# Second phase of a transformer kernel: the 64-row block of the MLP moved behind the scores, residual additions moved with it, one attention output a step later, one small exponential earlier

## The chip, the cores and the metric

The kernel runs on one core of one Trainium2 chip, as one launch. The metric is the device time in microseconds (us) of that core, the median of several runs. The core's engines are TensorE (PE in the profile, its weight loads PEld), VectorE (DVE), ScalarE (ACT), GpSimd (POOL) and SyncE (SP), which issues the DMAs.

## What is computed

The reference takes `x` of 8 x 1024 x 256 in float32 and adds two blocks to it, each on a layer norm of its input:

```python
x = x + attn(layernorm(x))          # latent attention, 16 heads, causal: first phase
x = x + ffn(layernorm(x))           # two layers of the following: second phase

def layer(x):
    q, k, v = split(shift_token(x) @ wqkv)            # 8 heads of 64
    q, k = rotary_xpos(l2norm(q) * qs, l2norm(k) * ks)
    x = x + local_attention(q, k, v) @ wo             # windows of 128, each sees itself and the one before
    h = layernorm(shift_token(x)) * lg + lb
    a, g = split(h @ w1 + b1)                         # 682 columns each
    return x + (a * gelu(g)) @ w2 + b2
```

The change touches the second phase alone, and there the order of work, not what is computed.

## The kernel before

The first phase (function `mla`) ends a little after 950 us of the span; the second (`local`) takes the rest.

**Passes, windows, chunks.** `local` goes through 16 passes (`passes`, L1049): two layers of eight batches. A pass has 8 windows of 128 tokens (attention works on these) and two chunks of 512 tokens (the MLP works on these), so there are 128 windows and 32 chunks.

**One loop of steps.** The order of PE, DVE, ACT and POOL is written out by hand: inside `tc.manual_schedule` (L1209) each of these engines does its instructions in the order of the program text. SP isn't in that list; its order is chosen when the program is built. The loop of L1210 makes one step per window, and in each step works on several windows at different stages (`each(step, name, back)` calls a method of the pass for the window `back` steps ago):

- `both` (L981, 4 back): on DVE, sums of the exponentials of a window and its predecessor, later added up over keys by PE;
- `qk` (L886, this window): PE multiplies into one of two double banks of PSUM, `pair`, that are taken in turn (`turns`, L869) by `qk` and by each of the two halves of `scores`; ACT squares (L897), DVE multiplies by tables (L899, L902), reduces (L908, L909), POOL adds and scales (L906, L911, L912);
- `transposes` (L923, 1 back): DVE turns 32x32 blocks (L930), and SP writes them to DRAM and reads them back as `qkT` (L933, L937);
- `v` (L915): PE, then a copy by ACT;
- a unit of the MLP, `next(units)` (L1227);
- `values` (L990, 4 back): PE forms `o` (L1003) and the sums `s` (L1011); DVE takes the reciprocal of `s` (L1015), a sum for a later test (L1019), the product `oT` (L1020) and another sum (L1024);
- `scores` (L945, 3 back): PE, with 64 rows of contraction and 32 columns per matmul (L962), in two halves; ACT takes the exponential of each half (L968); POOL masks (L970, L975). The last window of a pass has half as many columns;
- in every second step `output` (L1028, two windows, 6 and 5 back): PE multiplies by `wo` into `psw`, DVE adds to the residual `x_` (L1037), SP writes `y` (L1040, L1042) and after a whole chunk reads `h` back (L1047);
- another unit of the MLP (L1238).

**The MLP as a generator.** `mlp` (L1097) yields eight units a chunk, two of them per step, so a chunk takes four steps. Units 1 to 5 are `up` for a gate and a value (tile `ag`, PE, 64 matmul instructions), then the gelu by ACT (L1127) and the product `hid` by DVE (L1128). Unit 6 is `up` for the last 42 columns of both, with its gelu (L1137) and `rest_hid` (L1142), and the norm of the next chunk. Unit 7 (L1149 to L1173) multiplies by `w2` into two banks, `psy`: first 128-row matmuls from `hid` (160 instructions), then those of the 64-row block from `rest_hid` (32 instructions), whose two row halves serve the two banks; then DVE adds each bank to the residual `x_` (L1165), and SP writes it to `xs` (first layer), or DVE adds `x2` as well (L1171) and SP writes `out` (second layer). Unit 8 scales the next chunk's `d` by ACT (L1091). Unit 7 is always the first unit of its step. It stands ahead of `values`, and `output` stands behind `scores` in that same step, because both come every fourth and every second step.

**Buffers.** The pool of PSUM banks tagged `mm` has three (`psum3`, L673): `pv`, `ag`, `psy`, `psw` and `s` share them. `pair` has two, `acc` (for `o`) one. The bank of a tile is handed on once its readers are done.

**Streams.** In steps 3 to 7 of a pass, `ahead` (L1186) loads and turns the input of the next pass (`turneds`, L804, on DVE; eight `xT` DMAs on SP). In the first layer it also norms it.

Of the kernel before, what the change touches and what calls it, by code (L numbers as in the profile page):

```python
# [82 lines left out]
def preln_mla_local_kernel(  # L83
# [574 lines left out]
    def local(ctx: ExitStack, verdict):  # L658
# [212 lines left out]
        class Pass:  # L871
# [3 lines left out]
            def __init__(self, n, l, b, w, x_, xT):  # L875
                self.n, self.l, self.b, self.w, self.x_, self.xT = n, l, b, w, x_, xT
                self.y = ys[n % 3]
                self.hs, self.rot, self.vs, self.pts, self.oTs = {}, {}, {}, {}, {}

            def key(self, i):  # L880
                return f"{self.b}_{self.l}_{i}"
# [107 lines left out]

            def values(self, i):  # L990

                key, vs, pts, oTs = self.key(i), self.vs, self.pts, self.oTs
                blocks = [(i - 1, P)] if i else []
                blocks.append((i, 0))
                o = pacc.tile([P, 2, 2, P], F32, tag="acc", name=f"o{key}")
                s = psum.tile([P, 2, P], F32, tag="mm", name=f"s{key}")
                place = lambda j: 2 * (j % 2) + j // 2
                for g in range(2):
                    for a in range(2):
                        for m, off in blocks:  # L1000
                            for j in range(4):
                                h = 4 * g + j
                                nc.tensor.matmul(  # L1003
                                    o[32 * j : 32 * j + 32, g, a, :],
                                    vs[m][:, h * DH + a * 32 : h * DH + a * 32 + 32],
                                    pts[m][g][:, place(j), off : off + P],
                                    start=(m == blocks[0][0]), stop=(m == i),
                                )
                for g in range(2):
                    for j in range(4):  # L1010
                        nc.tensor.matmul(  # L1011
                            s[32 * j : 32 * j + 32, g, :], ones, self.sums[g][:, place(j), :], start=True, stop=True
                        )
                rs = p1.tile([P, 2, P], F32, tag="lrs", name=f"rs{key}")
                nc.vector.reciprocal(rs, s)  # L1015
                if i % 2 == 0:
                    oTs[i // 2] = p2.tile([P, 4, 2 * P], F32, tag="oT", name=f"oT{key}")
                at = self.n * NT + i
                nc.vector.tensor_reduce(stats[:, 1, at : at + 1], s, AX.XY, ALU.add)  # L1019
                nc.vector.tensor_tensor(  # L1020
                    oTs[i // 2][:, :, (i % 2) * P : (i % 2 + 1) * P].rearrange("p (g a) q -> p g a q", g=2),
                    o, rs.unsqueeze(2).to_broadcast([P, 2, 2, P]), ALU.mult,
                )
                nc.vector.tensor_reduce(stats[:, 0, at : at + 1], rs, AX.XY, ALU.add)  # L1024
                if i:
                    del vs[i - 1], pts[i - 1]
# [23 lines left out]
        made = {}  # L1050
        chunks = [(n, m) for n in range(len(passes)) for m in range(NCH)]
        ds, found = {}, {}

        def look_at_chunk(k):
            if k < len(chunks):
# [41 lines left out]
        def mlp():  # L1097


            w = load_mlp(0)  # L1100
            yield
            look_at_chunk(0)
            yield
            norm_chunk(0)
            turn_chunk(0)
            yield
            scale_chunk(0, w)
            for k, (q, n) in enumerate(chunks):
                l, b, x_ = made[q].l, made[q].b, made[q].x_
                key = made[q].key(n)  # L1110
                d = ds.pop(k)

                def up(i):
                    ps = psum.tile([P, CH], F32, tag="mm", name=f"ag{key}_{i}")
                    for c in range(2):
                        times(
                            ps.rearrange("p (s a t) -> p s a t", a=4, t=32), w["1"][:, c, i, :], d[:, c],
                            c == 0, c == 1,
                        )
                    return ps  # L1120

                hid = p1.tile([P, NF, CH], F32, tag="hid", name=f"hid{key}")
                for i in range(NF):
                    gate = up(2 * i + 1)
                    a = up(2 * i)
                    ge = p2.tile([P, CH], F32, tag="ge", name=f"ge{key}_{i}")
                    nc.scalar.activation(ge, gate, AF.Gelu, bias=w["b1"][:, 2 * i + 1 : 2 * i + 2])  # L1127
                    nc.vector.scalar_tensor_tensor(  # L1128
                        hid[:, i, :], a, w["b1"][:, 2 * i : 2 * i + 1], ge, ALU.add, ALU.mult
                    )  # L1130
                    if i + 1 == NF:
                        look_at_chunk(k + 1)
                    yield
                both = up(2 * NF)
                ge = p2.tile([P, CH], F32, tag="ge", name=f"ge{key}_{NF}")
                last = slice(2 * NF, 2 * NF + 1)
                nc.scalar.activation(  # L1137
                    ge[:REST], both[64 : 64 + REST], AF.Gelu, bias=w["b1"][64 : 64 + REST, last]
                )
                for g in range(2):  # L1140
                    cols = slice(CH // 2 * g, CH // 2 * (g + 1))
                    nc.vector.scalar_tensor_tensor(  # L1142
                        rest_hid[64 * g : 64 * g + REST], both[:REST, cols], w["b1"][:REST, last],
                        ge[:REST, cols], ALU.add, ALU.mult,
                    )
                norm_chunk(k + 1)
                turn_chunk(k + 1)
                yield
                if l + 1 == DEPTH:  # L1149
                    xt = load_x2(b, n)  # L1150
                sums = [psum.tile([P, 2, D], F32, tag="mm", name=f"psy{key}_{g}") for g in range(2)]
                for g, ps in enumerate(sums):
                    for t in range(2):
                        cols = slice((2 * g + t) * P, (2 * g + t + 1) * P)
                        for i in range(NF):
                            times(ps[:, t, :], hid[:, i, cols], w["2"][:, i, :], t == i == 0, False)
                for t in range(2):
                    for g, ps in enumerate(sums):
                        rows = slice(64 * g, 64 * g + 64)
                        times(  # L1160
                            ps[:, t, :], rest_hid[rows, t * P : (t + 1) * P], w["2"][rows, NF, :], False, t == 1
                        )
                for g, ps in enumerate(sums):
                    part = slice(ST * n + 2 * g, ST * n + 2 * g + 2)
                    nc.vector.tensor_tensor(x_[:, part], ps, x_[:, part], ALU.add)  # L1165
                    if l + 1 < DEPTH:
                        nc.sync.dma_start(xs[b][:, part], x_[:, part])
                    else:
                        rows = slice(n * CH + 2 * g * P, n * CH + (2 * g + 2) * P)
                        both = xt[:, 2 * g : 2 * g + 2]  # L1170
                        nc.vector.tensor_tensor(both, x_[:, part], both, ALU.add)  # L1171
                        nc.sync.dma_start(out[b, rows].rearrange("(t p) d -> p t d", p=P), both)
                yield  # L1173
                if k + 1 < len(chunks) and made[chunks[k + 1][0]].l > l:
                    w = load_mlp(l + 1)
                scale_chunk(k + 1, w)
                yield
# [24 lines left out]
        def each(step, name, back):  # L1202
            j = step - back
            if 0 <= j < windows:
                n, i = divmod(j, NT)
                getattr(made[n], name)(i)

        E = mybir.EngineType
        with tc.manual_schedule(engines={E.PE, E.DVE, E.Activation, E.Pool}):  # L1209
            for step in range(windows + LAG):  # L1210
# [12 lines left out]
                each(step, "transposes", 1)  # L1223
                if not late:
                    each(step, "v", 0)
                if step >= LAG:
                    next(units, None)  # L1227
                if NT - 2 <= i and step < windows:
                    ahead(n + 1)
                each(step, "values", 4)  # L1230
                each(step, "scores", 3)
                j = step - 6
                if 0 <= j < windows and j % 2 == 0:
                    made[j // NT].output(j % NT // 2)
                elif 0 <= j < windows - 1 and (j + 1) % (B * NT) == 0:
                    w["o"] = load_o(passes[(j + 1) // NT][0])
                if step >= LAG - 2:
# [5 lines left out]
                if i >= NT - 5 and step < windows:  # L1243
                    got = ahead(n + 1)
                    if got:
                        ready[n + 1] = got
            for _ in units:
                pass

        ok = p1.tile([P, 2, B * DEPTH * NT], F32, name="okl")  # L1250
        for m, top in enumerate((HIGH, 1 / LOW)):
# [612 lines left out]
```

## Time and profile before

| | us |
|---|---|
| median of 3 runs | 3276.89 |
| lowest, highest | 3273.80, 3278.76 |
| the profiled execution | 3275.27 |
| its span, first to last instruction | 3273.5 |

The mean TensorE clock granted was 0.993 of full speed. In the profile, PE's matmuls are pipelined and overlap, so that a block's own cost is read from its start to the start of the next block, not from its length. In the groups by line, the columns are: line, engine, operation, tiles written and read, shapes, count, then busy us and mean ns of one, then idle time of the engine just before such instructions and what ended it. In the waits, they are: who waited, for whom, us in total, times, longest. L670 is the helper `times`, which issues four matmuls of 32 columns each; its blocks are told apart by their tiles.

### The profile page before, as it was taken

To read this page: it belongs to the slowest core of one execution; us is meant where nothing else is said; L and a number is where in the kernel's file an instruction comes from. 1 tells how busy PE (TensorE), PEld (TensorE's weight loads), DVE (VectorE), ACT (ScalarE), POOL (GpSimd) and SP (SyncE) were. 2 spreads that over 40 slices of the span, in tenths; PEclk is the share of its full clock that TensorE was granted. 3 is DMA by queue.
4 is the path that set the end of the run, shared out by engine and by line. 5 is a ranking of instruction groups with operands and counts; after the bars stand their busy time and mean duration, and the time that the engine had idled before them with its cause. 6 is when DMAs were issued, how large, how long until landed. Compare 5 with 4: busy or idle time off the path is not lost.

```text
span 3273.5 us, 112729 instructions
## 1 busy us (share of the span) xinstructions
PE 3177.2 (97%) x50274; PEld 1456.0 (44%) x50274; DVE 2671.1 (82%) x3934; ACT 1712.5 (52%) x2055; POOL 1341.6 (41%) x1064
## 2 busy tenths in 40 slices
PE   7999999999987999999999999999999999999998
PEld 2434343443333445444445444444554444544454
DVE  4999989998987888887888877777877878787773
ACT  6888888888852343444443444444444444444441
POOL 1001000000018655565555555555555555555540
PEclk9999999999998999999999999999999999999999
DMA  4133223323333444544445445444544545454431
GB/s 128 43 95 85 56 75 78 85 53 81 98 98 104 108 129 118 142 111 122 131 115 135 120 131 144 120 130 142 144 131 130 133 122 134 134 140 126 114 106 59
DMA packets 389900, 364.21 MB, mean 111 GB/s; under 512 B 158703, under 2 KB 337310, under 8 KB 389278
## 3 DMA queue, kind: packets, MB, share of 16 engines
q1 hardware_dynamic: 387422, 354.51, 40.1%
q8 instruction: 397, 6.50, 0.8%
q10 hardware_dynamic: 1984, 2.41, 0.2%
q14 instruction: 97, 0.79, 0.1%
HBM read 165.96 MB, written 140.51 MB: 94 GB/s over the span
## 4 chain that ended last, share of the span: by engine, by line
PE 84%; DVE 6%; ACT 4%; DMA 3%; issue 2%; SPq 1%; POOL 0%; ACTq 0%; DVEq 0%; POOLq 0%
PE ag L670 17%; PE pair L670 13%; PE psy L670 9%; PE psw L670 7%; PE acc L488 7%; PE pv L670 6%; PE o L1003 6%; PE sc L455 5%; PE pair L962 4%; DVE pt L477 3%; PE s L1011 2%; PE psx L201 2%; PE psq L201 1%; PE psR L201 1%; ACT pt L463 1%
## 5 line engine op out<-in xcount | busy, mean ns | idle before, releaser
L477 DVE TENSOR_TENSOR pt<-pt,er 128x1024 f32<-128x1024 f32 x576 | 671.9, 1222 | 35.5 <-ACT pt L463 35.5
L670 PE MATMUL ag<-d,l 128*32 128x512 f32 x5632 | 639.8, 593 | 0.7 <-ACT d L1085 0.4
L906 POOL TENSOR_TENSOR t<-t,t 128x1024 f32<-128x1024 f32 x128 | 304.2, 2377 | 780.2 <-DVE t L902 780.2
L463 ACT ACTIVATE pt<-sc 128x1024 f32<-128x1024 f32 x576 | 561.0, 1032 | 115.4 <-PE sc L455 105.6
L968 ACT ACT_TABLE_LOAD x120 | 154.0, 1283 | 686.9 <-PE pair L962 686.8
L670 PE MATMUL pair<-l_qkv,xT 128*32 128x512 f32 x4096 | 468.3, 597 | 6.6 <-ACT pt L968 3.2
L126 POOL TENSOR_TENSOR rn<-ss,half 128x16 f32<-128x16 f32 x128 | 373.4, 2917 | 13.9
L488 PE MATMUL acc<-pt,v 128*32 128x512 f32 (+3 forms) x3072 | 345.6, 497 | 11.1 <-DVE pt L477 10.0
L670 PEld LDWEIGHTS ag<-d,l 128*32 128x32 f32 x5632 | 179.0, 110 | 384.0 <-issue 362.0
L897 ACT ACTIVATE sq<-pair 128x1024 f32<-128x1024 f32 x128 | 131.2, 1025 | 331.0 <-issue 256.0
L899 DVE TENSOR_TENSOR t<-pair,l_cos 128x1024 f32<-128x1024 f32 x128 | 156.3, 1221 | 155.1 <-ACT sq L897 154.8
L670 PE MATMUL psy<-l,hid 128*32 128x256 f32 x5120 | 282.1, 379 | 0.0
L670 PEld LDWEIGHTS pair<-l_qkv,xT 128*32 128x32 f32 x4096 | 132.6, 111 | 307.8 <-issue 252.5
L1128 DVE SCALAR_TENSOR_TENSOR hid<-ag,l_b,ge 128x512 f32<-128x512 f32 x160 | 115.9, 724 | 188.2 <-ACT ge L1127 164.5
L968 ACT ACTIVATE pt<-pair 128x1024 f32<-128x1024 f32 (+1 forms) x256 | 235.1, 969 | 56.4 <-PE pair L962 55.1
L912 POOL TENSOR_TENSOR t<-t,rn 128x1024 f32<-128x1024 f32 x128 | 245.4, 1918 | 10.0
L455 PE MATMUL sc<-q,k 32*128 32x512 f32 (+3 forms) x3072 | 245.2, 380 | 4.0 <-ACT pt L463 3.0
L1003 PEld LDWEIGHTS o<-pt,v 128*32 128x32 f32 x7680 | 212.8, 110 | 72.7 <-issue 68.9
L670 PE MATMUL pv<-l_qkv,xT 128*32 128x512 f32 x2048 | 244.1, 592 | 0.0
L670 PE MATMUL psw<-l_o,oT 128*32 128x256 f32 x4096 | 240.2, 386 | 0.1
L1003 PE MATMUL o<-pt,v 128*32 128x128 f32 x7680 | 235.6, 273 | 1.7 <-POOL pt L970 1.6
L420 POOL TENSOR_SCALAR_AFFINE_SELECT er<-er 128x128 f32<-128x128 f32 x64 | 39.1, 610 | 480.7 <-ACT er L418 480.7
(324 smaller groups left out, 4639.5 us busy)
## 6 DMA issues: line engine op xcount, KB each, us to landing
z<-turned SPq DMA_DIRECT2D x512, 128.0 KB, 2.8
qkT<-z SPq DMA_DIRECT2D x128, 512.0 KB, 3.9
y<-xs SPq DMA_DIRECT2D x128, 128.0 KB, 3.8
h<-y SPq DMA_DIRECT2D x32, 512.0 KB, 4.4
zx<-turneds SPq DMA_DIRECT2D x120, 128.0 KB, 2.8
xT<-zx SPq DMA_DIRECT2D x240, 64.0 KB, 2.9
zh<-turnedh SPq DMA_DIRECT2D x120, 128.0 KB, 2.3
d<-zh SPq DMA_DIRECT2D x30, 512.0 KB, 3.3
```

What stands on the lines that cost most here:

```text
L126: nc.gpsimd.tensor_tensor(out_, in_, half[:, :n], ALU.pow)
L455: nc.tensor.matmul(two[n // 2][:, n % 2, lo : lo + w], k[rows], q[rows, h], start=(h == 1), stop=(h == 0),)
L463: nc.scalar.activation(pt, sc, AF.Exp, scale=SCALE)
L477: nc.vector.tensor_tensor(t, t, er.to_broadcast([P, 1024 // w, w]), ALU.mult)
L488: nc.tensor.matmul(self.acc[g][32 * n : 32 * n + 32, q0 - c * 512 :], self.v[:, kb, h * VW : h * VW + 32], pts[n // 2][:, n % 2, lo : lo + w],
L670: nc.tensor.matmul(out[four], w[:, four], rhs, start=start, stop=stop)
L897: nc.scalar.activation(sq, qk, AF.Square)
L899: nc.vector.tensor_tensor(t1, qk, A[:, i].unsqueeze(2).to_broadcast([P, 2, HEADS, DH]), ALU.mult)
L906: nc.gpsimd.tensor_tensor(t1, t1, t2, ALU.add)
L912: nc.gpsimd.tensor_tensor(t1, t1, rn.unsqueeze(3).to_broadcast([P, 2, HEADS, DH]), ALU.mult)
L968: nc.scalar.activation(pt[:, :, : n * P], flat[:, :, : n * P], AF.Exp, scale=-1.0)
L1003: nc.tensor.matmul(o[32 * j : 32 * j + 32, g, a, :], vs[m][:, h * DH + a * 32 : h * DH + a * 32 + 32], pts[m][g][:, place(j), off : off + ...
```

## The change

Four edits, all in `local`:

1. Unit 7 issues only the 128-row matmuls of `psy`. The 64-row block, the residual additions and their DMAs go into a closure, `rest`, that the step calls behind `scores`.
2. `values` keeps its matmuls; its four DVE instructions become a method `divide`, called behind `rest`. So on DVE the residual additions still stand ahead of the reciprocal, but both now stand behind the scores' place.
3. In a step with a `rest`, `output` is held and called in the next step, behind `v` and ahead of the first unit.
4. Ahead of `scores`, ACT takes the exponential of one zeroed column, `spark`, that nothing reads.

```diff
+                self.done[i] = o, s
+
+            def divide(self, i):
+                key, vs, pts, oTs = self.key(i), self.vs, self.pts, self.oTs
+                o, s = self.done.pop(i)
                 rs = p1.tile([P, 2, P], F32, tag="lrs", name=f"rs{key}")
                 nc.vector.reciprocal(rs, s)
...
-                for t in range(2):
+                def rest(w=w, sums=sums, l=l, b=b, n=n, x_=x_, xt=xt):
+                    for t in range(2):
+                        for g, ps in enumerate(sums):
+                            rows = slice(64 * g, 64 * g + 64)
+                            times(
+                                ps[:, t, :], rest_hid[rows, t * P : (t + 1) * P], w["2"][rows, NF, :], False, t == 1
+                            )
                     for g, ps in enumerate(sums):
-                        rows = slice(64 * g, 64 * g + 64)
-                        times(
-                            ps[:, t, :], rest_hid[rows, t * P : (t + 1) * P], w["2"][rows, NF, :], False, t == 1
-                        )
-                for g, ps in enumerate(sums):
-                    part = slice(ST * n + 2 * g, ST * n + 2 * g + 2)
-                    nc.vector.tensor_tensor(x_[:, part], ps, x_[:, part], ALU.add)
-                    if l + 1 < DEPTH:
-                        nc.sync.dma_start(xs[b][:, part], x_[:, part])
-                    else:
...
+                        part = slice(ST * n + 2 * g, ST * n + 2 * g + 2)
+                        nc.vector.tensor_tensor(x_[:, part], ps, x_[:, part], ALU.add)
+                        if l + 1 < DEPTH:
+                            nc.sync.dma_start(xs[b][:, part], x_[:, part])
+                        else:
+                            rows = slice(n * CH + 2 * g * P, n * CH + (2 * g + 2) * P)
+                            both = xt[:, 2 * g : 2 * g + 2]
+                            nc.vector.tensor_tensor(both, x_[:, part], both, ALU.add)
+                            nc.sync.dma_start(out[b, rows].rearrange("(t p) d -> p t d", p=P), both)
+
+                rests.append(rest)
                 yield
...
+        column = p1.tile([P, 1], F32, name="column_l")
+        nc.gpsimd.memset(column, 0.0)
+        spark = p1.tile([P, 1], F32, name="spark")
...
                 if not late:
                     each(step, "v", 0)
+                while held:
+                    j = held.pop()
+                    made[j // NT].output(j % NT // 2)
                 if step >= LAG:
                     next(units, None)
                 if NT - 2 <= i and step < windows:
                     ahead(n + 1)
                 each(step, "values", 4)
+                if 0 <= step - 3 < windows:
+                    nc.scalar.activation(spark, column, AF.Exp)
                 each(step, "scores", 3)
+                full = bool(rests)
+                while rests:
+                    rests.pop()()
+                each(step, "divide", 4)
                 j = step - 6
                 if 0 <= j < windows and j % 2 == 0:
-                    made[j // NT].output(j % NT // 2)
+                    if full and step + 1 < windows:
+                        held.append(j)
+                    else:
+                        made[j // NT].output(j % NT // 2)
```

More of the change, by code (lines that the diff above doesn't have):

```diff
@@ L877, in __init__ @@
                 self.y = ys[n % 3]
-                self.hs, self.rot, self.vs, self.pts, self.oTs = {}, {}, {}, {}, {}
+                self.hs, self.rot, self.vs, self.pts, self.oTs, self.done = {}, {}, {}, {}, {}, {}
             def key(self, i):
@@ L990, in values @@
             def values(self, i):
-                key, vs, pts, oTs = self.key(i), self.vs, self.pts, self.oTs
+                key, vs, pts = self.key(i), self.vs, self.pts
                 blocks = [(i - 1, P)] if i else []
@@ L1052, in local @@
         ds, found = {}, {}
+        rests, held = [], []
         def look_at_chunk(k):
@@ L1148, in mlp @@
                 yield
-                if l + 1 == DEPTH:
-                    xt = load_x2(b, n)
+                xt = load_x2(b, n) if l + 1 == DEPTH else None
                 sums = [psum.tile([P, 2, D], F32, tag="mm", name=f"psy{key}_{g}") for g in range(2)]
@@ L1156, in mlp @@
                             times(ps[:, t, :], hid[:, i, cols], w["2"][:, i, :], t == i == 0, False)
-                for t in range(2):
-                    for g, ps in enumerate(sums):
-                        rows = slice(64 * g, 64 * g + 64)
-                        times(
-                            ps[:, t, :], rest_hid[rows, t * P : (t + 1) * P], w["2"][rows, NF, :], False, t == 1
-                        )
-                for g, ps in enumerate(sums):
-                    part = slice(ST * n + 2 * g, ST * n + 2 * g + 2)
-                    nc.vector.tensor_tensor(x_[:, part], ps, x_[:, part], ALU.add)
-                    if l + 1 < DEPTH:
-                        nc.sync.dma_start(xs[b][:, part], x_[:, part])
-                    else:
[L1169 to L1172, printed above, removed]
+                def rest(w=w, sums=sums, l=l, b=b, n=n, x_=x_, xt=xt):
[5 more added lines that the diff above has]
+                            )
+                    for g, ps in enumerate(sums):
+                        part = slice(ST * n + 2 * g, ST * n + 2 * g + 2)
[8 more added lines that the diff above has]
+                rests.append(rest)
                 yield
@@ L1246, in local @@
                         ready[n + 1] = got
+                while rests:
+                    rests.pop()()
             for _ in units:
-                pass
+                while rests:
+                    rests.pop()()
         ok = p1.tile([P, 2, B * DEPTH * NT], F32, name="okl")
```

## The prediction

> **What bounds the kernel now.** I read the page first (busy times, then the chain that ended last), then the groups of the second phase by shape, then the timeline of each engine around one step in which the down projection `psy` runs, then the waits.
>
> The page: TensorE (PE) is busy 97% of the span and makes 84% of the chain; VectorE (DVE) is next.
>
> ```profile
> PE 3177.2 (97%) x50274; PEld 1456.0 (44%) x50274; DVE 2671.1 (82%) x3934; ACT 1712.5 (52%) x2055; POOL 1341.6 (41%) x1064
> PE 84%; DVE 6%; ACT 4%; DMA 3%; issue 2%; SPq 1%; POOL 0%; ACTq 0%; DVEq 0%; POOLq 0%
> ```
>
> In the second phase PE issues almost without a hole, so only what makes its blocks start later than their own work demands can be won. The timeline of PE around the nineteenth `psy` (columns: start, length, engine, line, tile, count) shows two such places:
>
> ```profile
> 2417.68 1.92 PE L670 MATMUL ag<-d,l 128*32 128x512 f32 x16
> 2419.73 3.64 PE L670 MATMUL pair<-l_qkv,xT 128*32 128x512 f32 x32
> 2423.19 1.90 PE L670 MATMUL pv<-l_qkv,xT 128*32 128x512 f32 x16
> 2424.91 8.82 PE L670 MATMUL psy<-l,hid 128*32 128x256 f32 x160
> 2433.66 1.09 PE L670 MATMUL psy<-l,rest_hid 64*32 64x256 f32 x32
> 2434.68 1.95 PE L1003 MATMUL o<-pt,v 128*32 128x128 f32 x64
> ...
> 2437.00 1.32 PE L962 MATMUL pair<-qkT 64*32 64x160 f32 x64
> ```
>
> First, 16 matmuls take 1.72 us from start to next start (`pv`, 2423.19 to 2424.91), but the 16 of `ag` at 2417.68 take 2.05 until `pair` starts: 0.33 of waiting. The list of waits names the cause, ScalarE (ACT) reading the pair bank that `qk` will overwrite; the groups show what stands in front of that read:
>
> ```profile
> PEld pair L670 <- ACT pt L968: 37.3, 55, 1.3
> ```
>
> ```profile
> L968 ACT ACT_TABLE_LOAD x120 | 154.0, 1283 | 686.9 <-PE pair L962 686.8
> ```
>
> The table load queues behind the wait for the scores, so each of 120 steps pays 1.28 us between scores and exponential, though ACT was idle before (686.9 us in all).
>
> Second, `psy` runs in 128-row tiles, its rest in 64-row ones. At 53.65 ns a matmul (half of `pv`'s 107.3, for half the columns) 160 take 8.58 us; from `psy` to its rest are 8.75: 0.16 over. The rest's 32 run two row halves at a time, 26.8 ns each, 0.86; up to `o` are 1.02: 0.16 over. A change of tile shape costs about 0.16 each way.
>
> **What the Trainium skill says.** "TensorEngine Tiling (Array Packing)", Key Properties: changing the tiling mode drains TensorE. The trace agrees, with those 0.16 us. "ScalarE: Activation LUTs", What ACT_TABLE_LOAD costs: 1283 ns for the load plus some 1380 for a drain. The 1283 is here; the drain isn't: the load at 2437.93 is followed by the exponential at 2439.22, 1.29 later. "GPSIMD Engine Reference", Specifications: it shares SBUF interfaces with VectorE, and DVE instructions with two SBUF inputs contend. The trace agrees: the residual addition L1171 takes 0.69 us alone and 1.67 beside POOL's L912.
>
> **The change part by part.** There are 32 chunks, so 32 `psy` steps; the last two (of the drain-out) have no scores beside them.
>
> *Early exponential.* It adds one [128,1] exponential per step; the skill's price for an instruction with immediate operands (186 ns, same section; an estimate) makes 0.2 us. It stands after the gelu and ahead of the scores, where ACT idles 4 to 12 us, so it costs nothing; without that cover it would be 128 x 0.2 = 26. The load moves into the idle time and the exponential starts 1.28 earlier. On PE's path this counts only where `qk` waits for it: once per chunk, in the step after which only 16 `ag` matmuls follow the scores. I count 0.31 us (2.05 against 1.74, the shortest case) x 29 (the last such steps have no `qk` after them) = **9.0 us**. Elsewhere 3.4 us of `ag` or 3.5 of `psw` hide it.
>
> *64-row block behind the scores.* Scores are 64-row too, so rest and scores share one change in and one out: 0.16 + 0.16 = 0.33 x 30 = **9.9 us**. Between 0 (if something else makes those 0.16) and 0.35 per chunk; I take 0.33.
>
> *Attention output (`psw`, 64 matmuls) a step later.* The same work; `x_` and `y` get that half chunk 17 us later, and `h`, which reads `y`, waits for the other half, written two steps later. On SP, its two `y` issues move past the next step's four `z` and one `qkT`; the `xs`/`out` issues come with the additions, some 3 us later. The reader of `xs` is chunks away. 0. But `psw` no longer stands between scores and `qk`. Counting from the start of the scores, `qk` now comes at 1.07 + 1.02 = 2.10; the exponential releases the bank at 0.92 + 1.02 = 1.94, which without the early load would be 3.22. Covered, with 0.1 left.
>
> *Additions and reciprocals.* They now wait for the end of the rest. This is where I expect a new stall. DVE in the same step, before:
>
> ```profile
> 2434.79 0.69 DVE L1165 TENSOR_TENSOR xs<-psy,xs 128x512 f32<-128x512 f32 x1 [0.72 <-PE psy L670]
> 2435.51 0.69 DVE L1171 TENSOR_TENSOR x<-xs,x 128x512 f32<-128x512 f32 x1
> 2436.12 0.68 DVE L1165 TENSOR_TENSOR xs<-psy,xs 128x512 f32<-128x512 f32 x1
> 2436.84 1.67 DVE L1171 TENSOR_TENSOR x<-xs,x 128x512 f32<-128x512 f32 x1
> 2438.44 1.75 DVE L1015 RECIPROCAL rs<-s 128x256 f32<-128x256 f32 x1
> ...
> 2442.70 1.41 DVE L804 STREAM_TRANSPOSE turneds<-xs 128x256 f32<-128x256 f32 x4
> 2444.03 1.25 DVE L987 TENSOR_TENSOR both<-pt,pt 128x512 f32<-128x512 f32 x2
> 2446.63 1.23 DVE L899 TENSOR_TENSOR t<-pair,l_cos 128x1024 f32<-128x1024 f32 x1 [1.34 <-ACT sq L897]
> ```
>
> Set the old start of the rest (2433.66) to 0. After: `o` -0.16, `s` 1.58, scores 2.13, rest 3.21, `qk` 4.23, `pv` 7.66, `psw` 9.38, `ag` 12.83, `o` 16.27, the next `s` 18.01. DVE: additions from 3.21 + 1.13 (as 2434.79 stands to 2433.66) = 4.34; four at 0.61 to 0.72 end at 7.0 (L912, over at 4.3, no longer beside them); the four of `divide` 2.87, to 9.88; `turneds` 1.34; `both` 1.16, to 12.4; L899 to the transposes 6.06 (2446.63 to 2452.68), to 18.4; the held addition L1037 0.69, 19.1. The three banks named `mm` go round in turn: `pv`, `psy`, `psy`, `s`, then `pv`, `psw`, two `ag`, `s`. So that `s` takes `psw`'s bank and waits for L1037: 19.18 against 18.01, **1.17 us of stall** where before its bank was `pv`'s and free. Queued behind on PE is everything. This is the second layer with the `turneds` of the next stream: 6 chunks. Without `turneds` (second layer, 7 chunks; in 6 of them the scores are 0.2 shorter too) and in the first layer with them (two additions, 8 chunks) DVE is ready 0.15 ahead; in the rest of the first layer over 1 us ahead. Affine selects now run beside L1171; the page's neighbour for that, L794 beside a select 0.70 against 0.40, suggests +0.3. Bounds: 0 to 2.2 per such chunk; I take 1.17 + 0.3 = 1.47 x 6 = 8.8. In the one step whose `psw` can't be held it waits for the first addition's bank, 0.8. Sum **9.6 us**.
>
> *Sum.* -9.0 - 9.9 + 9.6 = -9.3. The profiled execution took 3275.27 (a span of 3273.5 and 1.8 around it), which becomes 3266.0. The median of the runs, 3276.89, stands 1.6 above it, so 3276.9 - 9.3 = **3267.6**.
>
> **The rivals.** *No new stall* (DVE keeps ahead, or the banks fall otherwise): 3276.9 - 18.9 = 3258. For: the slack is within 0.2 us in most chunks, DVE idles 0.7 to 1.3 in front of L1165, L1037 and L899. Against: the count for the second layer. *The drains only move*, or the stall eats the gain: with DVE 0.6 us later than counted, 6 x 1.77 + 15 x 0.44 + 0.8 = 18, so 3276.9 - 18.9 + 18 = 3276. *Slower*: one mechanism, the held L1037 behind a late DVE. It decides from 0.64 us of lateness beyond my count, where 6 x 1.81 + 15 x 0.48 + 0.8 reaches the whole gain of 18.9. If L1171 is blocked by the selects as it was by L912 (1.67 against 0.69, 1.0 once) and the divisions too slip by 0.3, the lateness is 1.3: 6 x 2.47 + 15 x 1.14 + 0.8 = 32.7, so 3276.9 - 18.9 + 32.7 = 3290.7. Against it: L1165, L1015 and L1020 read PSUM, and the trace shows them equally long beside selects. *The change doesn't do what it says*: SP's order is not written out by hand, and at the layer change (2033 to 2042) `qkT` already stalls PE 5.8 us; that could move by some 3 either way, which is in the range.
>
> **How the numbers follow.** Partial stall 0.44, its own range 3262 to 3272; no stall 0.25; gain eaten 0.20; slower 0.11. 0.2% is 6.6 us, about what a measurement of this kernel can tell from no change: faster is below 3270.3, slower above 3283.4. So faster 0.68, same 0.21, slower 0.11. The range from 3255 to 3279 leaves out the slower case and a little on the low side.
>
> **What would show it.** Right: table loads of L968 no longer waiting for `pair L962`; `ag` x16 to `pair` 1.74; `psy` followed by `o` after 8.59; scores and rest back to back; waits of PE `s` for DVE L1037 in the second layer, about 1.5 us each. Wrong: other shapes still 0.16 over, no wait at `s`, or waits of `s` in the first layer too.

## The result, and the profile after

| us | before | after |
|---|---|---|
| median of 6 runs each | 3275.72 | 3258.86 |
| lowest, highest | 3273.80, 3278.76 | 3258.18, 3261.64 |
| the profiled execution | 3275.27 | 3258.18 |
| its span | 3273.5 | 3256.5 |

The ratio is 0.9949, with a 95% interval from 0.9939 to 0.996: 16.9 us faster. The forecast was 3267.6. The time is inside the range, but it is the rival "no new stall" (3258) that came, not the likeliest case. That it comes within 1 us of that rival's figure is in part luck: the rival's 18.9 us measured 16.3 in its two terms; what happened elsewhere (below), 0.8 us in all, and a median before that is 1.2 lower here than in the three earlier runs nearly made up for it.

The page of the kernel after, its busy times and its chain:

```profile
PE 3161.7 (97%) x50274; PEld 1461.0 (45%) x50274; DVE 2650.2 (81%) x3934; ACT 1733.9 (53%) x2183; POOL 1344.1 (41%) x1065
PE 84%; DVE 8%; ACT 3%; DMA 2%; issue 1%; SPq 1%; POOL 1%; ACTq 0%; DVEq 0%; POOLq 0%
```

PE does the same 50274 matmuls and is still the bound. ACT has 128 instructions more (the `spark`s).

PE's timeline around the nineteenth `psy`, the step that the prediction showed:

```profile
2412.87 8.82 PE L670 MATMUL psy<-l,hid 128*32 128x256 f32 x160
2421.51 1.93 PE L1003 MATMUL o<-pt,v 128*32 128x128 f32 x64
...
2423.80 1.32 PE L962 MATMUL pair<-qkT 64*32 64x160 f32 x64
2424.91 1.07 PE L670 MATMUL psy<-l,rest_hid 64*32 64x256 f32 x32
2425.91 3.64 PE L670 MATMUL pair<-l_qkv,xT 128*32 128x512 f32 x32
2429.37 1.90 PE L670 MATMUL pv<-l_qkv,xT 128*32 128x512 f32 x16
2431.09 3.64 PE L670 MATMUL psw<-l_o,oT 128*32 128x256 f32 x64
2434.54 3.62 PE L670 MATMUL ag<-d,l 128*32 128x512 f32 x32
2437.97 1.93 PE L1003 MATMUL o<-pt,v 128*32 128x128 f32 x64
2439.72 0.62 PE L1011 MATMUL s<-both,ones_l 128*32 128x128 f32 x16
2440.27 1.32 PE L962 MATMUL pair<-qkT 64*32 64x160 f32 x64
```

Read from start to next start: `psy` to `o` 8.63 (it was 8.75 to the rest), scores to rest 1.11, rest to `qk` 1.00. The line to look at is `s` at 2439.72: it has no bracket, so it waited for nothing, 1.75 us after the start of `o`. Here the forecast had a stall of 1.47.

DVE beside it:

```profile
2426.02 0.69 DVE L1172 TENSOR_TENSOR xs<-psy,xs 128x512 f32<-128x512 f32 x1 [3.65 <-PE psy L670]
2426.75 1.14 DVE L1178 TENSOR_TENSOR x<-xs,x 128x512 f32<-128x512 f32 x1
2427.81 0.68 DVE L1172 TENSOR_TENSOR xs<-psy,xs 128x512 f32<-128x512 f32 x1
2428.52 0.99 DVE L1178 TENSOR_TENSOR x<-xs,x 128x512 f32<-128x512 f32 x1
2429.43 1.75 DVE L1021 RECIPROCAL rs<-s 128x256 f32<-128x256 f32 x1
...
2439.61 1.29 DVE L930 STREAM_TRANSPOSE turned<-t 128x512 f32<-128x512 f32 x2
2440.83 0.64 DVE L1043 TENSOR_TENSOR xs<-psw,xs 128x512 f32<-128x512 f32 x1
```

The held addition, L1043 now, starts at 2440.83, 1.1 us after `s` did. So `s` can't have used `psw`'s bank in this step. In the whole phase PE waits for a held addition twice:

```profile
PE ag L670 <- DVE xs L1043: 0.7, 1, 0.7
PE s L1011 <- DVE xs L1043: 0.3, 1, 0.3
```

One wait of 0.7 us at an `ag` and one of 0.3 at `s`, against a forecast of six of 1.47.

ACT's groups by shape show the early exponential:

```profile
L1248 ACT ACT_TABLE_LOAD x120 | 154.0, 1283 | 2.1
...
L1248 ACT ACTIVATE spark<-column_l 128x1 f32<-128x1 f32 x128 | 26.0, 203 | 1.4
```

The same 120 table loads of 1.28 us are now made by the `spark` line and wait for nothing (2.1 us in all, where L968's loads waited 686.9 for the scores). The `spark` costs 0.20 us, all of it in ACT's idle time. On PE, all 29 blocks of `ag` x16 ahead of a `qk` now take 1.741 us, where the median was 2.049.

**Where the 17.1 us of span went.** Per chunk, from the starts of PE's blocks in both traces: 0.308 at `ag` x16 (29 times: 8.9 us), and 0.25 at the shape changes (30 times: 7.4 us). That is 16.3. The rest is one place, the change of layers, where PE waits for `qkT`: about 3 us better in this pair of executions; against it stand some 1.5 us lost up to the twelfth window and 0.7 between windows 76 and 80.

### The profile page after: what moved, and what is told of

It is laid out like the page before. It is cut to its first block, busy times and chain, and to the rows that moved or that the text cites. A ratio compares the mean times of both kernels' runs of the same rounds, so it can differ in the third digit from the quotient of the medians.

```text
span 3256.5 us, 112852 instructions
## 1 busy us (share of the span) xinstructions
PE 3161.7 (97%) x50274; PEld 1461.0 (45%) x50274; DVE 2650.2 (81%) x3934; ACT 1733.9 (53%) x2183; POOL 1344.1 (41%) x1065
## 4 chain that ended last, share of the span: by engine, by line
PE 84%; DVE 8%; ACT 3%; DMA 2%; issue 1%; SPq 1%; POOL 1%; ACTq 0%; DVEq 0%; POOLq 0%
PE ag L670 18%; PE pair L670 12%; PE psy L670 9%; PE psw L670 7%; PE acc L488 6%; PE pv L670 6%; PE o L1003 6%; PE sc L455 5%; PE pair L962 4%; DVE pt L477 4%; PE s L1011 2%; PE psx L201 1%; PE psR L201 1%; ACT pt L463 1%; PE psq L201 1%
## 5 line engine op out<-in xcount | busy, mean ns | idle before, releaser
L968 ACT ACTIVATE pt<-pair 128x1024 f32<-128x1024 f32 (+1 forms) x256 | 235.2, 968 | 537.0 <-PE pair L962 496.4
L912 POOL TENSOR_TENSOR t<-t,rn 128x1024 f32<-128x1024 f32 x128 | 243.5, 1902 | 10.0
L1021 DVE RECIPROCAL rs<-s 128x256 f32<-128x256 f32 x128 | 223.1, 1743 | 15.8 <-PE s L1011 15.7
```

The source lines that it names most:

```text
L912: nc.gpsimd.tensor_tensor(t1, t1, rn.unsqueeze(3).to_broadcast([P, 2, HEADS, DH]), ALU.mult)
L968: nc.scalar.activation(pt[:, :, : n * P], flat[:, :, : n * P], AF.Exp, scale=-1.0)
```

## The experiments

Each kernel is compared with the kernel before on the same chip, as a ratio; "per chunk" is read from the starts of PE's blocks, as the mean over twelve chunks of the first layer and eleven of the second. Unless another kernel is named, the edit is made to the changed kernel.

**Without the spark.**

```diff
-                if 0 <= step - 3 < windows:
-                    nc.scalar.activation(spark, column, AF.Exp)
```

> The changed kernel without the early exponential; nothing else differs. Theory (the early load is what lets the output move away from behind the scores): in the 29 steps with 16 ag matmuls behind the scores the wait of 0.31 us returns (8.9), and in the 30 psy steps qk follows 2.1 us (i=6) or 1.95 us (i=2) after the start of the scores, while the bank is released at 0.92 + 1.28 + 1.02 = 3.22 or, with half-width scores, 0.92 + 1.28 + 0.60 = 2.80: 1.1 or 0.9 us each, 29.5 in all. Together +38: about 3297 us, slower than the kernel before. Rival (the early load is worth only the wait that the trace of before showed): +9, about 3268.

Measured: 3292.27, ratio 1.0041 [1.0026, 1.0057], a span of 3291.3. The other three edits alone are slower than the kernel before. PE's timeline at the same step, then its waits:

```profile
2447.21 1.07 PE L670 MATMUL psy<-l,rest_hid 64*32 64x256 f32 x32
2449.39 3.64 PE L670 MATMUL pair<-l_qkv,xT 128*32 128x512 f32 x32 [1.11 <-ACT pt L968]
```

```profile
PE pair L670 <- ACT pt L968: 25.0, 30, 1.1
```

The rest no longer covers the table load: `qk` waits 1.11 us for the exponential to release the pair bank. Rest to `qk` is 2.19 or 1.89 (full or half scores) against 1.00 and 1.08, and `ag` x16 is back at 2.05. Per chunk 1.26 and 1.19 over the changed kernel. So the spark is worth 35 us of span in this order (30 by the ratios; the theory had 38), not the 9 of its own term: the move of `psw` takes away the cover that had hidden the load.

**The spark alone**, in the kernel before: the same two lines and the column, ahead of `scores`.

> The kernel before with the early exponential alone. Theory: the 29 waits of 0.31 us behind 16 ag matmuls go and nothing else moves: -8.9, about 3267 against a before of 3276 in the same call. Rival (the earlier exponential also brings the masks and sums forward and so ends further waits): more than -12.

Measured: 3269.95, ratio 0.9977 [0.9969, 0.9985], about 7.5 us. Comparing block by block, the 29 `ag` blocks give 8.9 us, exactly the term of the sum. In the first layer 2.0 come back: in six chunks `psw`, behind the scores, waits 0.33 longer for the addition that frees its bank:

```profile
PEld psw L670 <- DVE xs L1165: 3.5, 6, 0.7
```

A PE that no longer waits for ACT meets a DVE that is late. So the spark without the other edits doesn't get the whole of its term.

**The attention output not held.**

```diff
-                    if full and step + 1 < windows:
+                    if False:
```

> The changed kernel with the attention output in its own step also where a rest was done, so behind the divisions. Theory: psw finds no bank free: pv's is taken by s, and the first psy bank is read by the residual addition, which ends 1.13 + 0.69 us after the start of the rest, while PE could start psw at about 1.0: a stall of 0.8 us in 30 steps, +24, about 3283. Rival (psw waits for something else or not at all; holding it is not needed): 0, about 3259.

Measured: 3291.11, ratio 1.0047 [1.0029, 1.0064], 30 to 32 us over the changed kernel. PE's waits:

```profile
PE psw L670 <- DVE xs L1172: 27.9, 29, 1.9
```

In place, `psw` directly follows the rest and needs a bank that the residual additions must free first: 1.0 us a time in this list, 1.15 with what the starts show, up to 1.9 in the first layer, where the norm of the next input stands ahead of the additions. The theory named the wait; its size was somewhat low. The hold, which costs the changed kernel 1.0 us of waits in all, is what makes the moved rest pay.

**Half of the rest left directly behind `psy`**, so that PE changes its tile shape twice more per chunk.

```diff
+                for g, ps in enumerate(sums):
+                    rows = slice(64 * g, 64 * g + 64)
+                    times(ps[:, 0, :], rest_hid[rows, :P], w["2"][rows, NF, :], False, False)
...
-                    for t in range(2):
+                    for t in (1,):
```

> The changed kernel with half of the 64-row block (t = 0) directly behind the 128-row matmuls of psy, as in the kernel before, and the other half behind the scores. The same matmuls; what comes back is one change of tile shape in and one out per chunk. Theory (each change drains): the 0.25 us per chunk that the two traces differ by here, up to the 0.33 that I had predicted, x 30 = +7.5 to +9.9, about 3267. Rival (the gain of these blocks came from elsewhere, such as the order against scores): 0, about 3259.

Measured: 3273.95, ratio 0.9989 [0.9981, 0.9997], 13 us over the changed kernel. Per chunk 0.43 and 0.47, but not all of it is shape: the 16 matmuls left behind the scores are too short a cover for the exponential,

```profile
PE pair L670 <- ACT pt L968: 4.4, 16, 0.5
```

which makes some 0.13 to 0.17 of it. What is left, about 0.3, is the price of the two changes, with `psy` to the rest at 8.747 again. (In chunks with half scores, where no such wait stands in the list, the starts give 0.23.) Some 3 us more were lost at the change of layers.

**The three banks strictly in turn**: what the prediction assumed.

```diff
+            def tile(self, shape, dt, tag, name):
+                self.n += 1
+                return banks.tile(shape, dt, tag=f"{tag}{self.n % 3}", name=name)
```

> The changed kernel with the three mm banks handed out strictly in turn, one buffer each, as the prediction had assumed; in the trace of the changed kernel s started 1.7 us before the held addition had ended, so it must have had another bank. Theory (the predicted stall is real where s gets psw's bank, and the build avoided it by giving s another): in the 6 chunks of the second layer with turneds, s waits from 2439.72 to the end of L1043 at 2441.41 + 0.06, so about 1.75 us each, +10.5, little elsewhere: about 3269, with waits of PE s for DVE L1043 in the trace. Rival (DVE's lateness costs nothing wherever the banks fall): 0, about 3259.

Measured: 3279.9, ratio 1.0002 [0.9994, 1.0011]: the whole gain is gone. (The class moves the lines behind L684 by 11: L1054 is the held addition.) PE's timeline, same step, and its waits:

```profile
2450.45 1.93 PE L1014 MATMUL o<-pt,v 128*32 128x128 f32 x64
2454.01 0.64 PE L1022 MATMUL s<-both,ones_l 128*32 128x128 f32 x16 [1.63 <-DVE xs L1054]
```

```profile
PE s L1022 <- DVE xs L1054: 14.2, 13, 2.4
```

Here is the forecast stall, 1.63 us, at the place and for the instruction that the prediction named; the six chunks that it named stall 1.1 to 2.4 us, 1.57 in the mean against its 1.47, and the second layer loses 10.5 us beyond the changed kernel. But the first layer loses 6.8 as well, with six stalls of 0.56 to 1.44, where the prediction had DVE 0.15 ahead. In the first of them PE starts the rest at 1166.41; then, DVE and PE:

```profile
1167.41 1.33 DVE L805 TENSOR_SCALAR xs<-xs,mvs,rstds 128x256 f32<-128x256 f32 x4
1168.67 1.27 DVE L1183 TENSOR_TENSOR xs<-psy,xs 128x512 f32<-128x512 f32 x2
...
1181.27 0.64 DVE L1054 TENSOR_TENSOR xs<-psw,xs 128x512 f32<-128x512 f32 x1
```

```profile
1181.97 0.64 PE L1022 MATMUL s<-both,ones_l 128*32 128x128 f32 x16 [0.56 <-DVE xs L1054]
```

The norm of the next pass's input (L805), 1.3 us, now stands ahead of the residual additions (L1183): the move behind the scores took them past `ahead` as well. They start 2.26 us after the rest, not 1.13. In four of the six chunks DVE has no gap from there to L1054 and the stall is 0.56 to 0.58; in the other two, with 0.77 and 1.44, the transposes L941 also wait 0.18 and 0.58 for a transfer.

**The divisions ahead of the rest.**

```diff
-                while rests:
-                    rests.pop()()
                 each(step, "divide", 4)
+                while rests:
+                    rests.pop()()
```

> The changed kernel with the divisions ahead of the residual additions on DVE, PE's order untouched. DVE sat idle 3.65 us ahead of L1172 in the psy step and the divisions, 2.9 us, would fall into that. Theory (the order of the two is of no use; the additions ahead of the reciprocals only make DVE late): DVE is done some 2.3 us sooner, the leftover waits at L1043 (about 2 us in all) go, and nothing new waits: -1 to -3, about 3257. Rival (the additions must come first because they release the two psy banks): pv of the next step waits for its bank, up to 1 us in 30 steps, +10 to +30.

Measured: 3266.51, ratio 0.9961 [0.9948, 0.9975]; a span 8.8 us longer than the changed kernel's. The theory fell. In the first layer it loses 0.54 per chunk:

```profile
PE s L1011 <- DVE xs L1043: 4.6, 6, 1.6
```

In this build `s` does have `psw`'s bank in these steps of the first layer, and it waits six times, in the chunks where the norm of the next input stands ahead of DVE's other work. The second layer loses nothing between windows 76 and 120. Whether the bank or the order of DVE's work was to blame is asked again below.

**The rest ahead of the scores.**

```diff
-                each(step, "scores", 3)
                 full = bool(rests)
                 while rests:
                     rests.pop()()
+                each(step, "scores", 3)
```

> The changed kernel with the 64-row block and its additions just ahead of the scores in place of just behind. The number of changes of tile shape is the same, and DVE gets the additions 1.1 us sooner. Theory (what the rest does behind the scores is also to cover the exponential): qk follows the scores directly at 1.25 (1.03 where they are half as wide), the bank comes free at 0.92 + 1.02 + 0.05 = 2.0 (1.57): stalls of 0.73 and 0.54, 19 us over 30 chunks, about 3278. Rival (only the shared tile shape counts): 0, about 3259.

Measured: 3271.35, ratio 0.9978 [0.9968, 0.9988], 9.5 us over the changed kernel (13.7 by span). PE's waits:

```profile
PE pair L670 <- ACT pt L968: 14.0, 28, 0.7
```

The tile shapes still lie side by side, but `qk` directly follows the scores and waits for the exponential: 0.75 and 0.43 us, per chunk 0.60 and 0.53. The theory had this stall, at 0.73 and 0.54, so its mechanism holds; the sum fell short of its 19 because the smaller stall is 0.1 less and the change of layers came out 2.4 better here. The rest behind the scores is worth more as a cover than as a matter of shape.

**Not held at the change of layers.**

```diff
-                    if full and step + 1 < windows:
+                    if full and step + 1 < windows and step != 62:
```

> The changed kernel with the output of the one psy step ahead of the layer change (step 62) in its own step. The lead over the kernel before grew there by 3.9 us within four steps. Theory (the held y issues let the writes and reads of the stream's blocks on SP's queue start sooner): the stall of the scores for qkT grows back from 2.4 to some 4 us or more and the lead falls by 3 to 4 there, 0.8 of it psw's own wait. Rival (the gain there comes from the other edits or is chance): the lead falls by 0.8 alone.

One execution: 3267.96. Between windows 60 and 80 it loses 4.2 us against the changed kernel, 3.7 beyond what its chunks lose elsewhere. The sum is the theory's, but the wait of the scores for `qkT` grew to 2.95 only, not to 4. And it shows less than it seems: the kernel with half of the rest left behind `psy` holds `psw` there too and loses 3.0 in the same way, and the next one 4.4.

**Banks by hand, `s` never in `psw`'s.** As with strict turns, but in the step after a held `psw`, `s` takes the gate's bank and the next `ag` takes `psw`'s.

```diff
+                kind = name.rstrip("0123456789_")
+                held = kind == "s" and self.last[-3:-2] == ["psw"]
+                bank = self.order.pop(1 if held else 0)
+                self.order.append(bank)
+                self.last.append(kind)
+                return banks.tile(shape, dt, tag=f"{tag}{bank}", name=name)
```

> The changed kernel with its three mm banks given out by hand: in turn, as in the run with strict turns, except that s in a step after a held psw always takes the bank of the gate's ag (released long before), and the next ag takes psw's. Theory (strict turns lost only by s standing in psw's bank): the 17 us that strict turns cost in the windows come back but for the layer change, so 3260 to 3265, and the wait of PE at s for DVE L1054 (here the line of the held addition) falls from 13 to at most one. Rival (one shared order of three banks costs by something else, such as psy or ag waiting): 3272 to 3280, with waits of PE at ag or pv for DVE or ACT in place of those at s.

Measured: 3265.65, just above the theory's 3260 to 3265; ratio 0.9956 [0.9943, 0.997], whose interval overlaps that of the changed kernel. Against the kernel with strict turns it is 15 us faster by the ratios. Outside the change of layers its windows take what the changed kernel's take, 0.25 us more over 48 windows of the first layer and 1.2 over 44 of the second. PE's waits (lines moved by 15):

```profile
PE s L1026 <- DVE both L1002: 4.9, 5, 2.2
...
PE ag L670 <- DVE xs L1058: 0.8, 2, 0.5
```

No `s` waits for the held addition L1058 any more; the first line is an older wait, which the changed kernel has too. The next `ag`, which now has `psw`'s bank, comes 1.8 us after `s` and waits twice, 0.8 in all. With DVE as late as before, the bank that `s` is given decides whether PE stalls there.

**The same banks, and the divisions ahead of the rest.**

> Banks as in the previous run, and the divisions issued ahead of the rest of the down projection with its additions. Theory (the earlier run with the divisions first lost only because s was given psw's bank in the first layer): no wait of PE at s, and within 2 us of the previous run, 3258 to 3266. Rival (the order of DVE's work itself costs, because the additions, and with them psw, come 2.9 us later): 4 to 9 us above the previous run, with waits of PE at psw for DVE L1165.

Measured: 3270.12, ratio 0.9976 [0.9966, 0.9985]; 4.5 us over the run before it by the medians, 6.6 by the ratios. PE's waits:

```profile
PE pv L670 <- DVE xs L1187: 7.3, 6, 1.2
```

`s` no longer waits for the addition, and yet the first layer loses 9.0 us against the changed kernel: now six `pv` wait, 1.2 us each, for the bank of a `psy` whose addition (L1187) stands behind the divisions. The rival is right in its sum and in its cause, and only named the wrong tile. With either map of banks that was run, this order of DVE's work costs the first layer 6.5 to 9 us; the bank decides which matmul meets it. In the second layer, between windows 76 and 120, neither run with the divisions first loses more than 0.2 us to the changed kernel. So additions ahead of reciprocals is the better order in the first layer, and in the second the two are alike.

## Why the prediction was right or wrong

**Early exponential: right.** 0.31 x 29 = 9.0 forecast, 0.308 x 29 = 8.9 measured, at no cost on ACT. What the prediction didn't say plainly is that the move of `psw` rests on it: "which without the early load would be 3.22" is the stall in each `psy` step of the run without the spark: by the starts 1.19 us with full scores, 0.81 with half.

**Shape changes: right, and a quarter too large.** 0.33 per chunk became 0.274 in steps with full scores and 0.222 with half. `psy` to `o` is 8.633 where 160 x 53.65 ns are 8.58: 0.05 stay. With half scores another 0.08 stays between the rest and `qk`. The mis-sized term is 9.9, which measured 7.4. "TensorEngine Tiling (Array Packing)", Key Properties, of the Trainium skill says that a change of mode drains PE; the trace agrees, with a price of some 0.11 to 0.14 each way (0.15 by the run with half of the rest left behind `psy`).

**The attention output a step later, at nothing: right** as far as the traces tell. The two terms above make 16.3 of the 17.1 us, and the held addition is waited for twice, 1.0 us in all; not holding it would cost 30. The cover of 0.1 us was enough: rest to `qk` is 1.00 with full scores, with no wait.

**The new stall: wrong, and this is the step that failed.** "The three banks named mm go round in turn" was taken from the order of the tiles, not from the kernel as built. The build hands the banks out in an order of its own. In the built program, of the 29 steps after a held `psw`, `s` has the gate's bank in 14 and `psw`'s in 15; the 14 are those with the next stream's transposes beside them, the very ones in which DVE is late, and in the other 15 DVE is early enough, but for one wait of 0.3. With the divisions ahead of the rest the build gives `s` `psw`'s bank in 23 of the 29, so a change of DVE's order alone changes the map. What rule it follows isn't shown, so that it spared the late steps is, for the prediction, luck. With the banks forced into turns the stall appears (1.57 us in the mean of the six chunks against 1.47), and with them forced the other way it goes. So for the second layer the count of time was good: counted from the rest, which the prediction put at 3.21, `s` comes at 18.02 where it had 18.01, and DVE was even later than counted, since the reciprocal behind the four additions starts at 7.73 and not 7.0. What it had wrong is the bank.

**The first layer "0.15 ahead": wrong too**, though it didn't show in the changed kernel. With strict turns `s` waited there as well, six times. The count put the additions 1.13 us after the start of the rest, as in the second layer, and left out that the norm of the next input now runs ahead of them (2.26 us); a wait of the transposes for a transfer adds to it in two of the six.

**The layer change: open.** It was put at 3 us either way. In the kernel before and the changed one, PE's timeline around it:

```profile
2035.48 0.94 PE L1011 MATMUL s<-both,ones_l 128*32 128x128 f32 x16 [0.70 <-DVE both L987]
2039.26 1.32 PE L962 MATMUL pair<-qkT 64*32 64x160 f32 x64 [2.85 <-DMA qkT<-z]
2040.51 5.35 PE L670 MATMUL psw<-l_o,oT 128*32 128x256 f32 x64
2045.68 2.76 PE L670 MATMUL ag<-d,l 128*32 128x512 f32 x24
```

```profile
2028.58 0.74 PE L1011 MATMUL s<-both,ones_l 128*32 128x128 f32 x16
2031.55 1.32 PE L962 MATMUL pair<-qkT 64*32 64x160 f32 x64 [2.23 <-DMA qkT<-z]
2032.80 3.66 PE L670 MATMUL psw<-l_o,oT 128*32 128x256 f32 x64
2036.28 3.82 PE L670 MATMUL ag<-d,l 128*32 128x512 f32 x32
```

The wait for `qkT` is 2.23 instead of 2.85, `s` doesn't wait its 0.70, and `psw` takes 3.48 from start to next start instead of 5.17. That last 1.7 us, about half of the difference, is the clock: in the kernel before, the granted clock stands at half for 3.4 us from 2040.68 on, within `psw`, and in the changed one it doesn't. Beyond what their chunks lose elsewhere, the other kernels stand between 2.4 us better (the rest ahead of the scores) and 4.4 worse (banks by hand) than the changed one at this place, the kernel before 3.1 worse, and in no order with whether `psw` is held. The kernel with banks by hand has the same text as the changed one but for the banks. The prediction put 5.8 us of stall there down to `qkT`; by the starts that is what PE loses there in all, 12.83 us from the `o` ahead of these lines (2032.85) to `ag` where the same blocks take 6.99 without waits, and the wait for `qkT` is 2.85 of it. No run shows what sets the waits there, and with them the clock; that it is how the transfers happen to fall is only a guess. Without them the gain would be about 14.

**The range.** The stall rested on one premise that no view of the profile shows, and that premise carried the difference between the two likeliest cases. A chance of 0.25 for "no stall" trusted it too far. The forecast's own range, down to 3255, is what kept the result inside it, not its sum.

## What to carry to other kernels

An edit's worth is that of the order it lands in: the early table load gave 7.5 us alone and 30 to 35 behind the moved `psw`, and the move without it lost; so ask of each moved block what it was hiding. A count of who waits for a PSUM bank is only as good as the map of banks: read from the built program which tile held the bank last, since the order of the tiles in the text doesn't tell it, and a reordering can change it. Where one text sets the order of every engine, a call that is moved passes what lies between on each of them: here the additions also went behind the norm of the next input, which only some of the steps have. The 64-row block behind the scores served twice: it covers the exponential (9.5 us lost with it ahead of them) and shares their tile shape (some 0.25 us per chunk).

## What the runs showed of the hardware

- The addition with two inputs in SBUF, 0.69 us alone and 1.67 beside POOL's L912, took 1.14 and 0.99 beside POOL's affine selects of L975, and 0.69 to 0.73 in chunks where only those of L970 lay beside it (0.85 in the mean of 32).
- At the change of layers PE waits for `qkT`, and the record of the granted clock shows half speed there in ten of the twelve kernels: for 3.4 us beside waits of 2.0 to 3.3 us (2.85 in the kernel before), and for 6.8 in two with waits of 2.9 and 3.2 (half of the rest left behind `psy`, and banks by hand). The changed kernel, with 2.23 us, has none, nor has the one with the rest ahead of the scores, with 0.33. "TensorE: Matmul & The Clock Gate", Part 1, of the Trainium skill says that a window of about 3.4 us without work halves the clock. The trace agrees with the length of the slow stretch, 3.4 and 6.8. It doesn't show that a wait as long as the window is needed: all of these are shorter. And since 1.96 us (the divisions ahead of the rest) and 2.25 (no spark) were enough where 2.23 was not, the length of the wait alone doesn't decide.
